# Layer 0 with y kept by channels, and an order drawn up in finer steps

## The chip, the core and the metric

The kernel runs on one core of a Trainium2 chip. A core has five engines with instruction queues of their own: TensorE (PE; its weight loads are shown apart as PEld), VectorE (DVE), ScalarE (ACT), GpSimd (POOL) and SyncE (SP), which issues the DMA transfers. Each engine works through its queue in the order of the program and waits on semaphores. The metric is the device time of one execution in microseconds (us).

## The reference

The input x has 8 images of 64 x 64 positions and 192 channels. Two layers follow one another, each of the form x + layer(groupnorm(x)). Layer 0, the only one that the change touches, is a state-space block. Cut to what matters:

```python
xs = x + dwconv2d(x)                        # 3x3, by channel
h  = layernorm(xs)
z, xBC, dt = split(h @ in_proj_w.T)         # 384, 384+64+64, 6
xBC = silu(causal_conv1d(xBC))              # 4 taps
y  = ssd(xm, softplus(dt), A, Bm, Cm)       # 6 heads of 64, state 64
y  = (y + xm * D_skip) * silu(z)
y  = y * rsqrt(mean(y * y) + 1e-5) * rms_w  # mean over the 384 channels
x2 = xs + y @ out_proj_w.T
x2 = x2 + dwconv2d(x2)
out = x2 + gelu(layernorm(x2) @ fc1_w.T + fc1_b) @ fc2_w.T + fc2_b
```

`ssd` is a recurrence along the 4096 tokens of an image, worked out by chunks. Inside a chunk, y is a masked matrix of Cm and Bm products, weighted with exp of differences of a running sum `cs`, times x*dt. From the chunks before comes Cm times the carried state times exp(cs). Layer 1 is a scan over four directions; its code is the same in both kernels.

## The kernel before

All numbers are float32. `layer0` (from line 249) works in 64 tiles of 512 tokens, 8 for each image, and a tile has 4 chunks of 128 tokens. Data lie mostly with channels on the partitions: 128 channels as one 128 x 512 block, and the other 64 channels as two strips of 64 partitions, one for each half of the tokens, in a 128 x 256 block.

**Order.** Layer 0 is written as generators (`conv1`, `norm1`, `mix`, `convolve`, `gate`, `steps_in_time`, `decays`, `powers`, `scores`, `turn`, `states`, `mixer`, `output`, `conv2`, `norm2`, `mlp` and others), each of which walks over the tiles. A generator yields steps: an engine, a planned duration (the "weight", in us), a function that issues the instructions, and a time when the input is ready. The class `Flow` (line 150) is a list scheduler that runs while the program is built. It keeps one clock for each engine and always takes the step that can start earliest, plus 0.01 us times the rank of its generator (`RANKS0`). `f.keep` then fixes that order for each engine. Buffers are slots that a generator takes and gives back: five PSUM banks "mm", three "sm", five buffers "e", one each of "xdt", "xw" and "yc". `LAG` is added to each step's end. A step on ACT that needs another table of functions costs `TABLE` = 1.3 us more in the plan, and `STAY` shifts its place in the choice. So the planned weights decide what the engines' queues look like, and the chip then runs that order with its own durations.

**The part around the change**, for a tile:

- `gate` (L672, L683): z and dt by tokens. The normalised h is the stationary operand (128 tokens), the weights move (390 columns: 384 of z, 6 of dt). `keep_gate` adds the bias to dt on DVE (L700) and applies SiLU on ACT (L703) for each chunk.
- `steps_in_time` and `rows_of`: the running sums `cs` by tokens, and, turned, as rows `csr`, which go to DRAM (`csd`, L777). `decays` (L792) loads them back spread over 128 partitions into `e` (128 x 768 a chunk). `powers` turns `e` into exp(-relu(cs_i - cs_j)) with six activations and one (L805, L810), and `scores` multiplies it with the masked products of Bm and Cm (L834).
- `turn`: x by tokens through three transposes (L852), times dt (`xdt`, L858) and times the weight for the state (`xw`, L862).
- `states`: the part of y from the carried state. Two matmuls with Cm stationary (L911) give it by tokens, and DVE scales it by exp(cs) into `t1` (L920, twice a chunk). Then the new state: two matmuls (L938) and two DVE operations (L951, L954).
- `mixer`: y by tokens in one PSUM bank. Three matmuls with x stationary add x*D_skip (L977), six with `e` stationary (128 x 128) and `xdt` moving (64 columns) add the heads (L980). DVE adds `t1` (L993) and multiplies with silu(z) (L996), and ACT squares with a row sum (L1004).
- `output`: the root of the mean square by tokens (L1023, L1024), scaling (L1033), three transposes a chunk back to channels (L1040), a copy into `yc` (L1049), the output projection (L1064, and L287 for the last 64 channels), and on DVE the sum with xs (L1073).
- `mix` (`halves_of_pair`, L277 and L281), `output`, and `mlp` (`rows_of_pair`, L267 and L268; fc2 in L1180 and L287) hand PE one step each for a pair of banks or a whole projection, of 1.4 to 5.33 us by the plan.

## Time and profile before

| what | us |
|---|---|
| three runs of the kernel | 22291.52, 22295.5, 22308.64 (median 22295.5) |
| the profiled execution, its own time | 22303.65 |
| its span, from the first to the last instruction | 22301.9 |
| layer 0, about 75 to 4310 us of the span | 4235 |
| busy in that stretch: PE, DVE, ACT, POOL | 3892.10, 3459.95, 3076.69, 622.15 |

The page gives shares of the whole span, and four fifths of the span are layer 1. So for this change the stretch of layer 0 is read by itself, and its sums are divided by 64 to get times for a tile. Busy time on PE contains stretches in which its clock was granted at half, and there the same matmul shows twice its duration. A "row" of the groups shows the busy time of all instructions of one line and shape and the mean duration of one. Since matmuls overlap, busy time divided by the count is less than the mean duration. A float32 matmul shows as two records.

### The profile page before, as it was taken

To read this page: it belongs to the slowest core of one execution; us is meant where nothing else is said; L and a number is where in the kernel's file an instruction comes from. 1 tells how busy PE (TensorE), PEld (TensorE's weight loads), DVE (VectorE), ACT (ScalarE), POOL (GpSimd) and SP (SyncE) were. 2 spreads that over 40 slices of the span, in tenths; PEclk is the share of its full clock that TensorE was granted. 3 is DMA by queue.
4 is the path that set the end of the run, shared out by engine and by line. 5 is a ranking of instruction groups with operands and counts; after the bars stand their busy time and mean duration, and the time that the engine had idled before them with its cause. 6 is when DMAs were issued, how large, how long until landed. Compare 5 with 4: busy or idle time off the path is not lost. (4 is left out here: it accounts for less than half of the span.)

```text
span 22301.9 us, 358177 instructions
## 1 busy us (share of the span) xinstructions
PE 20993.5 (94%) x122600; PEld 11023.1 (49%) x122600; DVE 20777.7 (93%) x23205; ACT 19864.1 (89%) x35400; POOL 16103.8 (72%) x13412
## 2 busy tenths in 40 slices
PE   8999999799999999999999999999999999999999
PEld 5555555445544554455445544554455445544554
DVE  7888888799999999999999999999999999999998
ACT  6777777599989998999899989998899889988998
POOL 1111111189968996899689968997899789977997
PEclk8999999899999999999999999999999999999999
DMA  2111111233333333333333333333333333333332
GB/s 57 53 53 48 53 49 50 66 99 95 92 100 102 92 93 103 100 93 94 100 101 95 95 97 103 95 94 94 106 94 93 93 109 93 95 91 109 95 95 75
DMA packets 1732538, 1957.50 MB, mean 88 GB/s; under 512 B 551472, under 2 KB 1077712, under 8 KB 1721488
## 3 DMA queue, kind: packets, MB, share of 16 engines
q1 hardware_dynamic: 1730704, 1934.58, 31.5%
q8 instruction: 963, 15.78, 0.3%
q14 instruction: 871, 7.14, 0.1%
HBM read 1318.69 MB, written 212.60 MB: 69 GB/s over the span
## 5 line engine op out<-in xcount | busy, mean ns | idle before, releaser
L1959 POOL TENSOR_TENSOR hs<-hs,cb 128x1024 f32<-128x1024 f32 x6144 | 14589.7, 2375 | 497.7 <-POOL cy L1957 5.4
L1945 DVE TENSOR_TENSOR_SCAN hs<-ea,cy,g 128x512 f32<-128x512 f32 x10752 | 12915.9, 1267 | 188.2 <-PE g L1929 164.8
L1903 ACT ACTIVATE ea<-dr,an 128x512 f32<-128x512 f32 x12288 | 8158.2, 712 | 455.5 <-DVE hs L1945 406.0
L1894 ACT ACTIVATE pw<-duT,bt 128x384 f32<-128x384 f32 x14304 | 7840.5, 604 | 12.1 <-DMA xo<-xt 6.1
L1974 PE MATMUL y<-hs,sel 128*64 128x512 f32 x24576 | 6635.5, 618 | 353.9 <-POOL hs L1959 335.0
L1929 PE MATMUL g<-ident,pw 128*128 128x128 f32 x43008 | 6099.6, 281 | 70.0 <-DVE hs L1945 26.6
L1929 PEld LDWEIGHTS g<-ident,pw 128*128 128x128 f32 x43008 | 4614.9, 141 | 2558.0 <-issue 1254.1
L1917 PEld LDWEIGHTS g<-dg,duT 128*64 128x64 f32 x24576 | 1556.8, 136 | 2062.7 <-issue 1503.1
L1957 POOL COPY cy<-hs 128x2 f32<-128x2 f32 x6144 | 1160.9, 189 | 1901.7 <-DVE hs L1945 1863.2
L1917 PE MATMUL g<-dg,duT 128*64 128x128 f32 x24576 | 2256.5, 282 | 178.7 <-DVE hs L1945 106.1
L1974 PEld LDWEIGHTS y<-hs,sel 128*64 128x64 f32 x24576 | 1234.2, 135 | 1564.6 <-issue 865.1
L1945 DVE TENSOR_TENSOR_SCAN hs<-ea,g 128x512 f32<-128x512 f32 x1536 | 1754.4, 1203 | 161.3 <-PE g L1929 114.6
L500 POOL TENSOR_TENSOR s<-s,sq 64x256 f32<-64x256 f32 x256 | 221.7, 866 | 1878.3 <-ACT sq L494 1839.1
L1413 DVE SCALAR_TENSOR_TENSOR xs<-pad,p,xs 128x2048 f32<-128x2048 f32 x384 | 899.8, 2350 | 130.7 <-ACT xs L1397 120.8
L1808 PE MATMUL p_dt<-xdbl,wd 13*128 13x512 f32 x1536 | 868.9, 646 | 94.8 <-DVE duT L1837 71.4
L1773 PE MATMUL p_d<-xc,wx 128*44 128x512 f32 x1536 | 797.5, 603 | 28.5 <-DMA xc<-xo 28.5
L1830 PEld LDWEIGHTS p_du<-ident,de 128*128 128x128 f32 x3072 | 324.6, 141 | 618.0 <-DVE de L1821 407.3
L1808 PEld LDWEIGHTS p_dt<-xdbl,wd 13*128 13x128 f32 x1536 | 226.7, 184 | 732.6 <-DVE duT L1837 292.7
L1837 DVE TENSOR_TENSOR duT<-p_du,ut 128x512 f32<-128x512 f32 x768 | 514.0, 670 | 2.0 <-PE p_du L1830 2.0
L1821 DVE SCALAR_TENSOR_TENSOR de<-spa,p_dt 128x512 f32<-128x512 f32 x768 | 509.4, 664 | 3.9 <-ACT spa L1816 3.9
L1816 ACT ACTIVATE spa<-spa 128x512 f32<-128x512 f32 x768 | 485.8, 632 | 24.4
L1830 PE MATMUL p_du<-ident,de 128*128 128x128 f32 x3072 | 502.6, 287 | 3.5 <-DVE de L1821 3.5
(305 smaller groups left out, 19724.3 us busy)
## 6 DMA issues: line engine op xcount, KB each, us to landing
cb<-cd SPq DMA_DIRECT2D x4096, 128.0 KB
dr<-de SPq DMA_DIRECT2D x3072, 128.0 KB
xc<-xo SPq DMA_DIRECT2D x256, 768.0 KB
dg<-dz SPq DMA_DIRECT2D x256, 512.0 KB
e<-csd SPq DMA_DIRECT2D x256, 384.0 KB
ut<-xo SPq DMA_DIRECT2D x128, 768.0 KB
ut<-xo SPq DMA_DIRECT2D x256, 384.0 KB
xo<-xs SPq DMA_DIRECT2D x48, 1024.0 KB
```

The source lines that it names most:

```text
L1413: nc.vector.scalar_tensor_tensor(xs, tap(d, h, j), kw[:, d, j : j + 1], xs, ALU.mult, ALU.add)
L1773: nc.tensor.matmul(st["p_d"][:44], wx[:, d, k], st["xc"][:, d], start=d == 0, stop=d == DT - 1)
L1808: nc.tensor.matmul(ps, st["wd"][32:45, d * 128 : d * 128 + 128], xds[s % 2][32:45], start=True, stop=True)
L1830: nc.tensor.transpose(pt[:, j * 128 : j * 128 + 128], st["de", d][:, j * 128 : j * 128 + 128], ident)
L1894: o(nc.scalar.activation(to, what, AF.Copy, scale=by))
L1903: nc.scalar.activation(ea[:, f], state[s]["dr", d][:, f], AF.Exp, scale=an[:, k, p, at : at + 1])
L1917: nc.tensor.matmul(gs[f][i * 64 : i * 64 + 64, j * 128 : j * 128 + 128], state[s]["duT"][:, j, (2 * d + f) * 64 : (2 * d + f) * 64 + 64], ...
L1929: nc.tensor.transpose(gs[f][:, j * 128 : j * 128 + 128], state[s]["pw", p, j][:, 2 * d + f].rearrange("p a b -> p (a b)"), ident,)
L1945: nc.vector.tensor_tensor_scan(rev(h[:, f]), rev(ea[:, f]), rev(g[f]), 0.0 if first(s) else state[s - 1]["cy"][:, p, d, f : f + 1], ALU.mu ...
L1957: o(nc.gpsimd.tensor_copy(st["cy"][:, p, d], h[:, :, last]))
L1959: o(nc.gpsimd.tensor_mul(h, h, bc(st["cb", p], 1, [128, 2, TT])))
L1974: o(nc.tensor.matmul(y[half[f]], sel, hc[:, f], start=p == ORDER[0] and k > 0, stop=p == ORDER[-1]))
```

## The change

Layer 0 now keeps y by channels from the start, and the planner is given finer steps and other numbers. For a tile:

- z is computed by channels like the other rows (`halves_of_pair` for the first 256 rows, `single` for the last 128 and, with h stationary, for the six columns of dt).
- y comes out by channels: for each head `xdt` is stationary (64 columns) and `e` moves (128 columns), two heads side by side on the two halves of the PSUM partitions. The part of the carried state is added in the same bank: the state is stationary (64 x 64), and `ec` moves, which is Cm times exp(cs). `ec` is loaded like `e` (two more DMAs a chunk, from exp(cs) that ACT adds to `csr`) and multiplied with Cm on DVE.
- x*D_skip is made on ACT (`cvd`, three operations a tile), and DVE adds it and multiplies with silu(z) straight into `yc`. The transposes, the scaling by tokens and the copies into `yc` go.
- The mean square is now over partitions: ACT squares half a tile, a matmul with ones sums, and Ln and Exp run on 128 x 512 (`ry`). Since it comes after the projection, DVE multiplies p_o with `ry` and then adds xs.
- PE steps of `mix`, `gate`, `output` and `mlp` are split (`in_parts`), and the six activations of `powers` are six steps.
- Planned weights, `LAG` (0.3 to 0.35), `STAY` (-0.7 to -0.98) and all ranks but four are other numbers, so the whole order of layer 0 is drawn up anew.

```diff
-    mlp=8, norm2=-26, conv2=18, output=-48, mixer=5, states=-10, turn=-21, scores=7, powers=41, decays=-99,
-    steps_in_time=-25, convolve=-14, mix=-3, gate=3, norm1=-15, conv1=16, inputs=3, statistics=46, stay=-0.7,
+    mlp=8, norm2=-13, conv2=15, output=22, mixer=-1, states=7, turn=-21, scores=7, powers=24, decays=274,
+    steps_in_time=-7, convolve=12, mix=37, gate=0, norm1=-15, conv1=-10, inputs=41, statistics=-112,
+    stay=-0.98,
...
+    def in_parts(parts, ready):
+
+        for weight, part in parts:
+            r = yield step("PE", weight, part, ready)
+            ready = 0.0
+        return r
...
+        of, weight, size = (rest_of, 0.46, 3) if few else (main_of, 0.89, 1)
+        return [(weight * size, lambda k=k: of(range(k, k + size))) for k in range(0, n, size)]
...
-                1.3,
+                1.75,
                 lambda: [
                     nc.gpsimd.tensor_add(s2[two[g], half[g]], s2[two[g], half[g]], sq[two[g]]) for g in range(2)
...
+                yield "take", "cvd"
+                cvd = got["cvd", T] = tp.tile([128, 3, TT], F32, name="cvd")
+                for i in range(3):
...
+                        lambda: [nc.scalar.activation(cvd[:, i], cv[:, i], AF.Copy, scale=v128["dsk"][:, i : i + 1])],
...
+                            out.append(nc.tensor.matmul(at, wia[:, cols], main(h)[:, half[g]], start=True, stop=False))
+                        for c in range(NQ):
+                            at = ps[c // 2][:, TB + c % 2 * NH : TB + c % 2 * NH + NH]
...
+                            out.append(nc.tensor.matmul(at, h[:, tk], wia[:, DIN : DIN + NH], start=False, stop=False))
...
+                    parts = ((2.6, single),) if last else halves_of_pair(ps, wia, wib, h, cols)
...
+            r = yield step("ACT", 0.24, lambda: [nc.scalar.activation(csr[:, 1], ps[: NQ * NH, :Q], AF.Exp)], None, "explog")
...
+                        out = [nc.sync.dma_start(out=e, in_=src)]
+                        for i in range(2):
+                            by = csd[c * NH + i : c * NH + NH : 2, 1].partition_broadcast(NS)
+                            out.append(nc.sync.dma_start(out=ec[two[i]], in_=by))
...
+                            "DVE", 0.49, lambda: [nc.vector.tensor_mul(ec, ec, bc(cm[:, tk], 1, [128, NH // 2, Q]))]
...
-                                nc.tensor.matmul(pi[i][:, :HC], queries[i][:, tk], st[two[i]], start=True, stop=True)
...
-                        for hd in range(NH):
-                            cs = slice(hd * HD, hd * HD + HD)
-                            f.keep(nc.tensor.matmul(py[:, cs], e[:, hd], xdt[:, cs], start=False, stop=hd == NH - 1))
...
+                        for j in range(3):
+                            for i in range(2):
+                                hd = 2 * j + i
...
+                                        py[two[i], j * 128 : j * 128 + 128],
+                                        xdt[:, hd * HD : hd * HD + HD],
+                                        e[:, hd],
...
+                                        py[two[i], j * 128 : j * 128 + 128],
+                                        st[two[i], j * HD : j * HD + HD],
+                                        ec[two[i], j],
...
-                    q = yield step("PE", 2.35, out)
+                    q = yield step("PE", 1.7, out)
...
+                    q = yield step("DVE", 0.5, lambda: [nc.vector.tensor_add(yc[:, :, tk], v(py), cvd[:, :, tk])], q)
+                    f.give("sm", q)
+                    q = yield step("DVE", 0.53, lambda: [nc.vector.tensor_mul(yc[:, :, tk], yc[:, :, tk], zs[:, :, tk])])
...
+            r = yield step("ACT", 0.83, lambda: [nc.scalar.activation(ysq, yc[:, :, half[g]], AF.Square)], r)
...
+                    nc.tensor.matmul(ps[:, half[g]], ones1, ysq[:, j], start=j == 0, stop=j == 2) for j in range(3)
...
+                            lambda: [nc.vector.tensor_mul(inner[at], im(ps[at, : n * WI]), im(ry[at, tk]))],
...
+                        "DVE", (0.64, 0.38)[i], lambda: [nc.vector.tensor_add(inner, inner, im((main, rest)[i](xs)))]
```

## The prediction

> **What bounds the kernel now.** I read the sums of busy time by stretches first, because the page mixes two layers. Columns: stretch, length, then busy us (and instructions) of PE, PEld, DVE, ACT, POOL, then the granted PE clock, DMA share, GB/s.

> ```profile
> 75.00:4310.00 4235.00, 3892.10 (x18524) 2272.61 (x18523) 3459.95 (x7131) 3076.69 (x6233) 622.15 (x1049) 0.92 0.17 49
> 500.00:4200.00 3700.00, 3416.43 (x16395) 1990.03 (x16396) 3071.76 (x6325) 2723.93 (x5520) 553.89 (x928) 0.93 0.17 50
> 4300.00:4400.00 100.00, 61.61 (x209) 29.86 (x208) 64.95 (x47) 47.13 (x51) 3.33 (x8) 0.77 0.38 119
> ```

> Layer 0 takes 4235 us, 66.2 for each of 64 tiles. In a tile PE is busy 60.8, DVE 54.1, ACT 48.1, POOL 9.7. PE bounds, but loosely: it idles 5.4 us a tile, and its clock averages 0.92. The timeline of PE shows what the clock does (start, duration, line, records; in brackets the idle time before):

> ```profile
> 2024.92 2.82 PE L980 MATMUL p_y<-xdt,e 128*128 128x64 f32 x12 [0.76 <-DVE e L834]
> ...
> 2048.07 0.83 PE L977 MATMUL p_y<-dsk,cv 128*128 128x128 f32 x6
> 2048.74 1.45 PE L980 MATMUL p_y<-xdt,e 128*128 128x64 f32 x12
> 2050.12 0.28 PE L867 MATMUL p_b<-ident,bm 64*128 64x64 f32 x1
> ...
> 2051.11 2.81 PE L287 MATMUL p_f<-m,wf 128*64 128x256 f32 x24
> ...
> 2065.26 1.99 PE L277 MATMUL p_x<-h,wia 128*128 128x256 f32 x8
> 2067.18 1.13 PE L281 MATMUL p_x<-h,wib 64*128 64x256 f32 x8
> 2068.24 1.12 PE L474 MATMUL ln_m<-x,ones 128*128 128x512 f32 x2
> ```

> The six heads take 1.45 us at one time and 2.82 at another, shortly after an idle time of 3.23 us (before L741 at 2021.41): PE works at half rate now and then. At 0.92 of the clock, 60.8 busy us hold about 56 of full-rate work. So three terms make the period: 56 us of work, 5 lost to half rate, 5 idle. Idle time comes from the others, and DVE in turn waits for PE (who waits for whom, DVE, 500 to 4200 us: total us, times, longest):

> ```profile
> DVE xdt L858 <- PE p_y L980: 162.1, 84, 5.5
> DVE st L954 <- PE p_n L938: 53.1, 44, 4.3
> DVE h L482 <- PE ln_m L476: 51.6, 45, 5.9
> DVE t L920 <- PE p_i L911: 40.0, 37, 4.7
> DVE cv L636 <- ACT cv L621: 39.2, 20, 11.0
> ```

> All lines of that view with a PE step on the right add to 507 us, 9.1 a tile, three quarters of DVE's idle 12.1. The two engines hold each other up in a fixed order, with PE the longer.

> **PE, part by part** (full-rate durations, as distances between starts in the timeline).

> y and the carried state go first. Now a chunk costs 2.05 (2048.07 to 2050.12) and 0.48 for the two L911 products (four records, 0.16 apart by pairs); the other PSUM step of `states` stays. After: three pairs with 64 stationary columns and 128 moving. The nearest row is L287, pairs of the same shape with 256 moving columns: 24 records, six pairs, 2.74 us to the next start, so 0.457 a pair and 0.23 for 128 columns. Three pairs of heads are 0.69. Pairs for the state (64 rows to 64 columns) have no row: between 0.23, both at once, and 0.43, one after the other (a 128-column matmul is half of L476's 0.43 for 256). I take 0.23, as in L281 and L287 where halves of the array run together. The sum is 1.38, and 1.5 with a tail: 1.0 saved a chunk, 4.1 a tile. The other end is 2.1 to 2.3, which saves 1 to 1.8.

> The transposes L1040 go: 142.2 us of busy time for 256 chunks, 0.56, at full rate 0.5; 2.0 a tile.

> z: now two pairs of 2.45, 4.9. After, one pair as in `mix`, 2.98 (2065.26 to 2068.24), and `single`: half of that for its four 256-column matmuls, 1.49, and eight tiny ones. Four have 128 stationary columns, as L741, whose starts lie 0.22 apart: 0.88. The four strips I put at 0.15 (0.05 to 0.22): 0.6. Sum 5.95, so 1.05 more (0 to 1.3).

> The sums of squares are new: six 256-column matmuls of 0.43 as L476, 2.6 more.

> Sum: -4.1 - 2.0 + 1.05 + 2.6 = **-2.45 us of PE work a tile**, bounds -3.9 and +0.2. Splitting steps issues no instruction more.

> **DVE.** These rows carry it:

> ```profile
> L920 DVE TENSOR_TENSOR t<-p_i,dec 128x192 f32<-128x192 f32 x496 | 172.0, 351 | 45.2 <-PE p_i L911 43.9
> L996 DVE TENSOR_TENSOR yt<-yt,zs 128x384 f32<-128x384 f32 x248 | 152.5, 615 | 0.8
> L1073 DVE TENSOR_TENSOR xx0a<-p_o,xs 128x512 f32<-128x512 f32 x22 | 15.2, 692 | 41.3 <-PE p_o L1064 41.2
> L1073 DVE TENSOR_TENSOR xx0b<-p_o,xs 128x256 f32<-128x256 f32 x22 | 9.3, 424 | 8.4 <-PE p_o L287 8.3
> ```

> L920 goes, 172.0/64 = 2.7. `ec` times Cm has the shape of L996: 0.49 (half of L834, 980 ns) to 0.615, four times, 2.1. Behind the projection there was one sum, 0.69 + 0.42; after, a product in three pieces, 0.69 + 2 x 0.42, and then the sum: 1.5 more. dt: two additions for four, 0.15 less. The others keep their shapes. Net **+0.8: DVE 54.9**.

> **ACT.** Away: scaling 158.2, copies 121.8, squares with their sums 182.3, roots 32.2, in all 494.5/64 = 7.7. New: three `cvd` of about 0.7 (0.618 for 384 elements in L1033), two squares of 0.84 (as L810), Ln and Exp 1.3 (L512, L513), a second Cm 0.63, exp 0.25, z 0.2: 6.2. Net -1.5, ACT 46.6. A fall in `STAY` lets the planner change tables sooner; one load more a tile (1.28 us, 5.5 now) stays under ACT's 18 us of slack.

> **The rest at nothing, and its cover.** SP issues eight DMAs more a tile, 0.37 each as in L792, and two more chunk loads bring half as many bytes again; ACT waits 28.1 us for `e` in 56 tiles now, and if every wait doubled that is 0.5 a tile on ACT's slack, or 32 us in all without it. POOL's copies of the `cin` head wait for the banks of the tile before; POOL is busy 15%, and `mix` alone is queued behind. "mm" gives one bank to the squares for about two chunks; "sm" is taken five times a chunk instead of eight. `yc` has one buffer and is now taken at the start of `mixer`: the next tile's DVE sums queue behind this tile's last projection matmul, about 4 us of PE once in 66, against three more tiles' work in other generators. Who would be late if that shows is DVE, which is the rival below.

> Finer steps and new ranks have no row: they can save part of the 5.4 idle and the 5 at half rate, or add to them. The planned weights move towards the rows (POOL's sums 1.3 to 1.75, shown 2 x 0.866; its copies 0.8 to 1.05, shown 2 x 0.517), which speaks for a small gain. I take none.

> **Forecast**: 2.45 x 64 = 157 off the profiled execution's 22303.65, 22147; the median lies 8 lower, so **22140**. It holds if idle time and half rate stay as they are. Own range 22060 to 22230. Chance 0.43.

> **Rivals.**

> - *More.* With PE less loaded and in pieces, a quarter to a third of DVE's 9.1 goes too, 2.5 more a tile: 4.9 x 64 = 314 off, 21980. For it: four of the five longest waits end in a PE step. Against: xdt has one buffer still. 0.13.
> - *Half the gain goes to the clock.* From 0.923 busy to 0.616 the mean clock goes from 0.93 to 0.77, 0.5 of clock for each 1.0 of busy share. If PE's freed time turns to idle, 58.4 of 65 us busy instead of 60.8 of 66.2, the clock falls by 0.01, which is 0.7 us, and with some idle left 1.2 of 2.45 remain: 77 off, 22220. 0.12.

> [...]

> - *Nothing is left.* If the state pairs run one after the other (0.43 each) and the tiny matmuls cost 0.22, y is 2.2 and z 6.2: PE keeps 56 us, and the time is 22280. 0.12.

> [...]

> - *Slower: DVE takes over.* Place: its queue around xdt, y and the projection. If its waits are not shortened by PE's relief, because xdt and yc have one buffer each and their chain is the same length, the period is DVE's 54.9 + 12.1 = 67.0, 0.8 more: 51, or 22350 beside the median. It decides once PE's period, 66.2 less its saving, falls under that sum, which it does with any saving at all; so it hangs on the waits alone. For it: DVE at 83% of the period is close behind. Against: most of its waits name PE steps that get shorter. A badly drawn order would show here too. 0.20.

> **Range and chances.** 0.2% is about what a measurement can tell from no change, 45 us. More, forecast and the half gain are faster: 0.68, less 0.02 for the edges; nothing left is 0.13, slower 0.21. The range must take in the first rival and most of the last: 21960 to 22370.

> **What would show it.** Layer 0's end near 4155 in place of 4310. Right: y's busy time a chunk (2.58 now with both rows) falls to about 1.7; the state pairs start together; DVE's sum is 3510 in layer 0; PE's clock stays 0.92. Wrong if the state pairs start 0.1 us apart or more, if DVE idles 12 us a tile with PE's share under 0.88, or if ACT's waits for `e` exceed 2 us a tile. Layer 1, about 17990 us, must not move.

## The result and the profile after

The changed kernel takes 21974.96 us (median, 21962.79 to 21974.97), the kernel before 22298.75 in the same comparison: a ratio of 0.9853, interval 0.9836 to 0.987. That is 324 us less, where 155 were forecast. The profiled execution has a span of 21972.1 us.

Busy time of the changed kernel in layer 0, which now ends at 3982 us (columns as in the prediction):

```profile
75.00:3982.00 3907.00, 3614.18 (x20489) 2095.71 (x20487) 3527.94 (x6944) 3024.08 (x5667) 617.53 (x1049) 0.97 0.25 66
```

A tile takes 61.0 us instead of 66.2. PE's clock averages 0.97 where it was 0.92, and DVE is busy 90% of the time (it was 82%). The rest of the span is 17990 us, before 17993: all of the difference is in layer 0. The waits of DVE in the changed kernel, 500 to 3900 us:

```profile
DVE xdt L917 <- PE p_y L1013: 97.1, 97, 5.0
DVE h L503 <- PE ln_m L497: 49.1, 44, 4.4
DVE st L980 <- PE p_n L963: 12.3, 17, 4.3
DVE gm L885 <- PE p_g L881: 11.2, 17, 4.4
DVE yc L1042 <- PE p_y L1024: 10.7, 7, 5.1
```

All lines of that view with PE on the right add to 217 us in 55.7 tiles, 3.9 a tile instead of 9.1. Now the new y on PE, in the timeline of the changed kernel:

```profile
2033.80 0.88 PE L1013 MATMUL p_y<-e,xdt 128*64 128x128 f32 x12
2034.60 0.87 PE L1024 MATMUL p_y<-ec,st 64*64 64x128 f32 x12
2035.40 1.98 PE L304 MATMUL p_f<-m,wf 128*128 128x512 f32 x4
```

Heads and state take 0.80 each from start to start, 1.6 a chunk.

To compare versions I split a tile of layer 0 into three terms of PE, from all its records and the granted clock at each moment: **work** (busy time times clock), **half-rate loss** (busy time times one minus the clock) and **idle** time. The three add up to the period. Some matmul records are missing, so differences of 0.3 us in work mean little. The terms are rounded one by one.

| kernel | median us | period | work | half-rate loss | idle | DVE busy |
|---|---|---|---|---|---|---|
| before | 22298.75 | 66.2 | 56.4 | 4.5 | 5.4 | 54.1 |
| changed | 21974.96 | 61.0 | 54.8 | 1.7 | 4.6 | 55.1 |

Of the 5.1 us less, only 1.6 are work. 2.8 are half-rate loss and 0.8 idle time.

### The profile page after: what moved, and what is told of

It reads as the page before. It is cut to its first block, busy times and chain, and to the rows that moved or that the text cites. A ratio compares the mean times of both kernels' runs of the same rounds, so it can differ in the third digit from the quotient of the medians.

```text
span 21972.1 us, 362013 instructions
## 1 busy us (share of the span) xinstructions
PE 20709.3 (94%) x124584; PEld 10850.2 (49%) x124584; DVE 20850.1 (95%) x23026; ACT 19801.9 (90%) x34834; POOL 16081.9 (73%) x13412
## 5 line engine op out<-in xcount | busy, mean ns | idle before, releaser
L862 ACT ACTIVATE e<-e,cst 128x128 f32<-128x128 f32 x1536 | 567.2, 393 | 36.2 <-DMA e<-csd 34.4
```

The costliest lines, as they stand in the source:

```text
L862: nc.scalar.activation(e[:, h], e[:, h], AF.Relu, bias=cs[:, c, h : h + 1], scale=-1.0)
```

## The experiments

Three theories were tested. WORK: the time follows PE's work. ORDER: it follows the order that the planner draws (finer steps, ranks, weights). And, formed from the first eight runs, STREAM: PE's clock follows how long columns stream, and y by channels streams better. By streaming I mean the time that a matmul's moving columns take, without waits for weights. Ratios are to the kernel before, timed on the same chip as each group of versions (medians 22300.28, 22304.9, 22302.51 and 22301.08).

**Less work in the same order**

```diff
-                        for i in range(3):
-                            cs = slice(i * 128, i * 128 + 128)
-                            f.keep(nc.tensor.matmul(py[:, cs], cv[:, i, tk], dsk[:, i], start=i == 0, stop=False))
```

> The kernel before, same order on every engine, without the three matmuls a chunk that add x*D_skip (the output lacks that term). PE has 4 x 0.67 = 2.7 us of full-rate work less a tile, more than the change takes away (1.6 by the two traces). Theory WORK (one for one, as the prediction's sum): 64 x 2.7 = 171 less, about 22130. Theory DOUBLE (less work also wins back half-rate time): 300 or more less, under 22000. Theory ORDER (the waits are fixed by the order and the freed time turns into idle time): less than 80 off, 22220 to 22300, with PE's idle time a tile up from 5.3 towards 8 us.

Measured: 22237.95 us, ratio 0.997 (0.996 to 0.9981). Its busy times in layer 0:

```profile
75.00:4240.00 4165.00, 3759.57 (x16985) 2114.19 (x16982) 3455.50 (x7128) 3071.55 (x6233) 622.33 (x1049) 0.91 0.17 50
```

Work falls by 2.7 to 53.6 us a tile, and the period by 1.1: idle time rises to 6.3 and half-rate loss to 5.1. WORK and DOUBLE fall. The time is within what ORDER named, though idle time rose to 6.3 and not towards 8. In this order, 62 of the 171 us of work taken away reach the time; the rest went to idle time (1.0 a tile) and to half rate (0.6).

**Parts of the change, with the ranks that are at hand.** Finer steps alone, in the kernel before:

```diff
-                    p = yield step("PE", (5.33, 2.7)[i], project, r)
+                    p = yield from in_parts(sums_of(ps, wf2, m, 6, i), r)
```

> The kernel before with y by tokens, its own ranks and planned weights, but the PE steps of mix, the output projection, fc1 and fc2 and the six ReLUs of powers as separate steps. No instruction is added or removed. Theory ORDER by finer steps: 150 to 250 off, 22050 to 22150, and the half-rate time of a tile falls from 10 to 7 us or less. Theory WORK: no change but for the chance of another order, 22240 to 22360.

Measured: 22522.3, ratio 1.0099 (1.0084 to 1.0114). Both theories missed: the kernel got slower by 222 us. Half-rate loss is 5.3, idle time 7.3.

Coarse steps again, in the changed kernel:

```diff
-        for weight, part in parts:
-            r = yield step("PE", weight, part, ready)
-            ready = 0.0
+        r = yield step("PE", sum(w for w, _ in parts), lambda: [i for _, part in parts for i in part()], ready)
```

> The changed kernel with its ranks and weights, but each pair or projection on PE and the six ReLUs again as one step. Same instructions as the changed kernel. Theory ORDER by finer steps: 150 to 250 of the 324 are lost, 22120 to 22230. Theory WORK: it stays near 21975, within 60.

Measured: 22434.9, ratio 1.0061 (1.0044 to 1.0077), 460 us above the changed kernel and far outside both expectations. Its busy times in layer 0 hold the instructions of the changed kernel in 4360 us instead of 3907, with 9.8 us of idle time and 4.0 of half-rate loss a tile:

```profile
75.00:4435.00 4360.00, 3732.19 (x20488) 2188.89 (x20486) 3551.19 (x6943) 3097.39 (x5726) 612.12 (x1049) 0.92 0.22 59
```

The old ranks in the changed kernel:

```diff
-    mlp=8, norm2=-13, conv2=15, output=22, mixer=-1, states=7, turn=-21, scores=7, powers=24, decays=274,
+    mlp=8, norm2=-26, conv2=18, output=-48, mixer=5, states=-10, turn=-21, scores=7, powers=41, decays=-99,
...
```

> The changed kernel with finer steps and its weights, but the ranks and STAY of the kernel before. Same instructions but for the number of table loads. If the new ranks carry the gain, 100 or more are lost: 22080 and up. If finer steps or less work carry it, within 60 of 21975.

Measured: 22277.77, ratio 0.9991 (0.9981 to 1.0). 303 of 324 us are lost with the same work, as expected if the ranks carry the gain. So no part with borrowed ranks gives a clear gain: two of the three versions are slower than the kernel before, by 222 and 135 us. This does not yet say that finer steps are worth anything: the ranks of one plan were used in another.

**The same parts, each with ranks of its own.** I searched ranks for each set of steps until the planner's own plan was shortest, and ran the result, one search for each version. The edit is the dictionary of ranks alone, besides what is named.

> The changed kernel with coarse steps again, and with ranks of its own, found by a search for the shortest plan of these steps. Same instructions as the changed kernel. If finer steps are needed for the gain: 22060 to 22160. If any steps do once the ranks are drawn for them: within 50 of 21975, and the coarse run with borrowed ranks (22435) was slow for its ranks alone.

Measured: 22000.19, ratio 0.9864 (0.9847 to 0.988). Coarse steps with ranks of their own are 25 us behind the changed kernel; the rest of the coarse run's 22435 came from its ranks.

> The kernel before (y by tokens, coarse steps) with the planned weights and LAG of the changed kernel for the steps that both have, and ranks found by the same search. If better weights and a new search carry the gain: 22150 or less. If y by channels is needed: 22230 to 22330.

Measured: 22221.77, ratio 0.9961 (0.9947 to 0.9976), between the two expectations and 8 us from the second: new weights and a search give 83 us, not the whole gain.

> The kernel before (y by tokens) with finer steps, the new planned weights and ranks found by the search for these steps. If finer steps carry the gain once they have ranks of their own: 22100 or less. If y by channels is needed too: 22250 to 22400, still under the 22522 of finer steps with borrowed ranks.

Measured: 22273.06, ratio 0.9987 (0.9978 to 0.9996). With y by tokens, finer steps bring nothing; this order is 51 us slower than the coarse one at 22222.

To tell the search from the weights in the run at 22222:

> The kernel before with its own planned weights and LAG, and ranks found by the search from its own as a start. It separates the search from the weights in the run with both (22222). If the search carries those 80: 22210 to 22240. If the weights nearer to the trace do: 22270 to 22310.

Measured: 22203.51, ratio 0.9955 (0.994 to 0.997), a little under what the search was expected to carry.

> The kernel before with the new planned weights and LAG, but its old ranks. If weights nearer to the trace help by themselves: 22220 to 22270. If ranks fit only the weights that they were drawn for: 22350 to 22550, as in the runs with borrowed ranks (22278, 22435, 22522).

Measured: 22358.39, ratio 1.0026 (1.0016 to 1.0036). So the search alone gives 98 us, with the old weights. Weights nearer to the rows gave nothing here: with old ranks they cost 57 us, and with searched ranks the run that has them is 18 us slower (22222 against 22204).

> The changed kernel with seven ranks a little different (decays 154 for 274, mix 36 for 37, inputs 43 for 41, statistics -111 for -112), whose plan is as long as its own within 0.03%. It shows how far orders with the same work and the same length on paper lie apart on the chip. If the plan's length carries the time: within 15 of 21975. If orders scatter: 30 or more off, and then 25 us for finer steps (22000 against 21975) says nothing.

Measured: 21970.31, ratio 0.9852 (0.9837 to 0.9866). The edit changes the four ranks that are named, not seven. This neighbour lies within 5 us. But it is a near copy of one order, and two searches can end further apart: with y by tokens, searched orders lie at 22204, 22222 and 22273, and there the finer steps are the slowest. So it is not shown that the 25 us come from finer steps.

**What y by channels adds.** With searched ranks on both sides and coarse steps, y by tokens takes 22203.51 and y by channels 22000.19: 203 us, 3.1 a tile. The version by channels also has the new planned weights and LAG, which gave nothing above; with them on both sides the difference is 222 us. Work differs by 1.5 of the 3.1, half-rate loss by 1.6 (3.6 against 2.0), idle time by nothing (4.9 and 4.8). Layer 0 by tokens, then by channels:

```profile
75.00:4209.00 4134.00, 3821.36 (x18522) 2249.71 (x18521) 3438.71 (x7128) 3091.18 (x6250) 607.61 (x1049) 0.94 0.18 50
75.00:4008.00 3933.00, 3623.96 (x20534) 2135.67 (x20532) 3578.11 (x6946) 3024.91 (x5682) 629.56 (x1051) 0.96 0.25 66
```

Why does the clock differ at equal idle time? In layer 0 of both kernels' traces the granted clock is recorded as 1.00 or 0.50, and every stretch at one value is a multiple of 3.41 us long (174 records before, 106 in the changed kernel). Four stretches of 3.41 us of the kernel before, and PE's timeline in them:

```profile
1480.38:1483.79 3.41, 2.74 (x16) 1.61 (x14) 3.38 (x7) 3.38 (x8) 0.33 (x2) 1.00 0.00 0
1483.79:1487.20 3.41, 2.14 (x15) 1.84 (x15) 2.16 (x5) 2.29 (x8) 0.00 (x0) 1.00 0.00 0
1487.20:1490.62 3.42, 1.32 (x5) 0.85 (x5) 3.39 (x9) 0.88 (x3) 0.00 (x0) 0.50 0.00 0
1490.62:1494.03 3.41, 3.41 (x5) 1.34 (x5) 1.83 (x4) 3.39 (x6) 0.00 (x0) 0.50 0.00 0
```

```profile
1484.15 1.55 PE L980 MATMUL p_y<-xdt,e 128*128 128x64 f32 x12 [0.67 <-DVE e L834]
1485.63 0.27 PE L867 MATMUL p_b<-ident,bm 64*128 64x64 f32 x1
1486.81 0.49 PE L825 MATMUL p_g<-cm,bm 64*128 64x128 f32 x2 [0.91 <-DVE xw L862]
1488.83 0.88 PE L1040 MATMUL p_u<-ident,yt 128*128 128x128 f32 x3 [1.53 <-DVE yt L993]
```

PE is busy for 2.14 of 3.41 us in the second stretch, and the clock is halved behind it (0.50 after 1.00). Most of that busy time is L980, which moves 64 columns behind 128 weight columns: 12 records of 64 columns stream for 0.65 us (an estimate, 0.84 ns a column and record, from the 12 records of 512 columns of L1180 in the 5.15 us between 2042.06 and 2047.21), out of 1.48. I counted such streaming time for all stretches of 3.41 us between 500 and 4200 us (3880 in the changed kernel) that had the full clock:

| | before: stretches, then halved | changed |
|---|---|---|
| columns stream under half of the stretch | 84, 63 | 39, 35 |
| more | 852, 8 | 899, 6 |
| PE busy for 0.5 to 0.75 of it | 91, 42 | 53, 5 |

At the same busy share the kernel before loses its clock in 42 of 91 cases and the changed one in 5 of 53. Streaming separates the cases in both; busy time does so less well.

These counts add up the columns of matmuls that run side by side, such as L287's, whose pairs start 7 ns apart. Counted once, as the time in which any column streams, the separation is sharper. Under 0.4 of the stretch, 65 of 72 are followed by half rate in the kernel before and 39 of 44 in the changed one; above it 6 of 865 and 2 of 895. Over the traces of all seventeen versions, under 0.4 it is 970 of 1036, and from half of the stretch on 1 of 14340. The 0.4 was chosen after the counts, to divide these stretches; so divided, 156 of all 15993 lie on the wrong side, and 414 if they are divided by busy time, at the share (0.56) that suits the two kernels best.

To try streaming by itself, y by tokens was made to stream more and save nothing:

```diff
-                            cs = slice(hd * HD, hd * HD + HD)
+                            cs = slice(hd // 2 * 128, hd // 2 * 128 + 128)
```

> The kernel before, same order and number of instructions, but each head's matmul in y moves 128 columns instead of 64 behind the same 128 weight columns: the columns of both heads of a pair, so that y also gets products of one head with the other's x (that is what the output has wrong). Nothing is saved; PE streams 6 x 64 columns more a chunk, under its weight loads. Theory STREAM (the clock is halved after windows in which columns stream for less than about half of the time, and weight-bound matmuls count as little): half-rate loss falls from 4.5 us a tile to 3 or less, and the time by 60 to 200, to 22100 to 22240. Theory IDLE (the clock goes by the idle time between matmuls): no gain, 22290 to 22400.

Measured: 22236.2, ratio 0.997 (0.9959 to 0.9982). In its timeline and its sums:

```profile
2022.36 0.83 PE L977 MATMUL p_y<-dsk,cv 128*128 128x128 f32 x6
2023.03 1.50 PE L980 MATMUL p_y<-xdt,e 128*128 128x128 f32 x12
2024.46 0.28 PE L867 MATMUL p_b<-ident,bm 64*128 64x64 f32 x1
```

```profile
75.00:4240.00 4165.00, 3819.17 (x18515) 2230.84 (x18515) 3452.34 (x7126) 3072.60 (x6233) 618.18 (x1048) 0.95 0.17 50
```

The step is no shorter (1.43 us to the next start, before 1.38), the columns are twice as many, idle time stays (5.4 both times), and half-rate loss falls from 4.5 to 3.0. The kernel gets faster by 66 us while PE does more arithmetic. STREAM holds in this run, at the small end of what it named, and IDLE falls. Stretches at half rate go down from 146 of 1083 to 102 of 1054.

> The same edit in y by tokens with the new weights and its own searched ranks (22222). Theory STREAM: 22020 to 22160, most of the way to y by channels with coarse steps and its own ranks (22000). Theory IDLE: 22210 to 22320.

Measured: 22170.32, ratio 0.994 (0.9927 to 0.9954), against 22221.77: 51 us. Half-rate loss 2.8 (4.2). The direction holds, the size was guessed too large: set against the 222 us between 22222 and 22000, streaming more columns in the heads' step gives about a quarter. The rest is 1.6 us of work a tile and another 0.8 of half-rate loss, for which I have no run. The transposes and the state products, which the change also takes away, were not tried one by one.

**Who sets the period now**

```diff
-                    q = yield step("DVE", 0.23, lambda: [nc.vector.tensor_mul(gm, pg[:, :Q], up)], q)
+                    q = yield step("DVE", 0.23, lambda: [nc.vector.tensor_mul(gm, pg[:, :Q], up) for _ in range(2)], q)
```

> The changed kernel, same order, with the product of scores and mask done twice on DVE: 4 x 0.284 = 1.14 us of DVE work a tile more, 73 in all. If DVE sets the period of the changed kernel: 60 to 110 later, 22035 to 22085. If PE or the fixed order does: 30 or less.

Measured: 22004.73, ratio 0.9865 (0.985 to 0.988): 30 of 73 us.

```diff
+                    nc.tensor.matmul(ps[:, half[g]], ones1, ysq[:, 0], start=True, stop=True)
+                ]
+                + [
                     nc.tensor.matmul(ps[:, half[g]], ones1, ysq[:, j], start=j == 0, stop=j == 2) for j in range(3)
```

> The changed kernel, same order, with the first of the three matmuls of each half's sum of squares done twice: 2 x 0.43 = 0.86 us of PE work a tile more, 55 in all. If PE still sets the period one for one: 22020 to 22040. If DVE and PE share it, as 1.14 us more on DVE (30 of 73) suggests: 15 to 35 later, 21990 to 22010.

Measured: 22006.95, ratio 0.9866 (0.9851 to 0.9881): 32 of 55 us. DVE passes on 0.4 of what it is given and PE 0.6. Neither sets the period alone.

```diff
-("xdt", 1), ("xw", 1)
+("xdt", 2), ("xw", 2)
```

> The changed kernel with two buffers each for xdt and xw instead of one, and ranks found by the same search for these slots. The longest wait of DVE (xdt for p_y) goes. If the plan's gain of about 1% of layer 0 reaches the chip: 21920 to 21950. If the clock or DVE eats it: 21960 to 22000.

Measured: 21967.57, ratio 0.9849 (0.9835 to 0.9862), 7 us under the changed kernel, no more than `after_near` without second buffers. DVE's longest wait did not go:

```profile
DVE xdt L917 <- PE p_y L1013: 110.1, 77, 4.9
DVE h L503 <- PE ln_m L497: 26.8, 31, 4.3
```

Why it stayed with a second buffer was not followed up. No version here beats the changed kernel clearly.

The terms of all versions, in us a tile, sorted by time:

| version | median us | period | work | half-rate loss | idle | DVE busy |
|---|---|---|---|---|---|---|
| changed, two buffers, own ranks | 21967.57 | 61.0 | 54.9 | 1.7 | 4.3 | 55.5 |
| changed, near ranks | 21970.31 | 61.0 | 54.8 | 1.7 | 4.5 | 55.1 |
| changed, coarse, own ranks | 22000.19 | 61.4 | 54.6 | 2.0 | 4.8 | 55.9 |
| changed, more DVE | 22004.73 | 61.4 | 54.9 | 1.7 | 4.8 | 56.2 |
| changed, more PE | 22006.95 | 61.6 | 55.6 | 1.7 | 4.3 | 55.2 |
| tokens, own ranks and new weights, wide | 22170.32 | 64.0 | 56.2 | 2.8 | 5.0 | 54.0 |
| tokens, own ranks, old weights | 22203.51 | 64.6 | 56.1 | 3.6 | 4.9 | 53.7 |
| tokens, own ranks, new weights | 22221.77 | 64.9 | 55.9 | 4.2 | 4.8 | 54.0 |
| before, wide | 22236.2 | 65.1 | 56.7 | 3.0 | 5.4 | 53.9 |
| before, no skip term | 22237.95 | 65.1 | 53.6 | 5.1 | 6.3 | 54.0 |
| tokens, finer, own ranks, new weights | 22273.06 | 65.9 | 56.7 | 3.5 | 5.7 | 53.5 |
| changed, old ranks | 22277.77 | 65.8 | 54.7 | 3.7 | 7.4 | 55.5 |
| before, new weights | 22358.39 | 67.0 | 56.3 | 4.6 | 6.1 | 53.9 |
| changed, coarse | 22434.9 | 68.1 | 54.3 | 4.0 | 9.8 | 55.5 |
| before, finer | 22522.3 | 69.6 | 57.0 | 5.3 | 7.3 | 53.9 |

## Why the prediction was right in sign and wrong in size

The failed step is the one that carried the forecast: "It holds if idle time and half rate stay as they are", with "Finer steps and new ranks have no row [...] I take none". What was set at zero there measured 3.6 us a tile (2.8 of half rate, 0.8 of idle time), 230 us. It is not all the order's doing. Along the path of runs at the end of this section, half rate goes from 4.5 to 3.6 with a new search, to 2.0 with y by channels and to 1.7 in the changed kernel. The prediction had no clock term for y itself. The term that I did size, PE's work, was too large: 1.6 and not 2.45. The two errors have opposite signs, so that the forecast still named about half of the gain is partly luck; had the work alone counted, the gain would have been about 100 us at best, and the run without the skip term shows that even this is not passed on in a given order.

By the steps:

- *PE's terms.* y costs 1.6 a chunk (1.5 taken). The squares and z cost more. By busy time a tile, the little half-rate time included, the squares take 196.7 us in 64 tiles, 3.1 (2.6 taken), and z 6.4 (5.95 taken): its rows sum to 125.7 + 72.7 + 70.3 + 45.0 + 61.0 + 32.6 = 407.3 us. Two of these rows of the changed kernel:

```profile
L1069 PE MATMUL p_q<-ysq,ones 128*128 128x256 f32 x768 | 196.7, 393 | 9.2 <-ACT ysq L1057 9.0
L706 PE MATMUL p_z<-h,wia 128*128 128x256 f32 x256 | 70.3, 394 | 2.3 <-ACT m L1173 1.9
```

- *Bounds.* The sum's upper bound of +0.2 does not follow from the ends that it names: -1 for y, -2.0 for the transposes, +1.3 for z and +2.6 for the squares make +0.9.
- *Signs.* y's busy time fell to 1.74 us a chunk, the state pairs start together and DVE's sum is 3528, as named. The clock did not stay at 0.92: it rose to 0.97, and that is the step above.
- *DVE*: 54.9 forecast, 55.1 measured; the product of `ec` takes 601 ns, as L996 did (615). *ACT*: 46.6 forecast, 47.3 measured. *The cover*: ACT waits 33.9 us for `e` in 55.7 tiles (28.1 in 55.9 before). These held.
- *Rival "more"* gave the right time, 21980, by luck, and half of its mechanism: DVE's waits for PE fall by 5.2 us a tile, twice what was priced, while the work that it adds them to was too large. Pieces are not the reason: with coarse steps and ranks of their own the waits are 3.0 us a tile. Nor are searched ranks alone: with y by tokens they leave 8.5 of 9.1. Nor is y by channels alone: with old ranks 5.8 remain. The waits fall where y by channels and ranks of its own come together.
- *Rival "half the gain goes to the clock"* had the sign wrong for this change. PE's busy share stayed (0.92 and 0.93) and the clock rose. The slope that I took from 0.77 at 0.616 mixed the end of layer 0 with its middle. The run without the skip term does go that way: less work, more half-rate loss.
- *Rival "nothing is left"*: the state pairs take 0.80 us for three, as the heads' pairs do, and the two of a pair start 7 ns apart, so they run together: 0.27 us a pair, while they write two halves of the partitions of one bank; one after the other would be 0.43, by an estimate from the 256 columns of L476. The rival's time was wrong by its own figures too: y at 2.2 a chunk and z at 6.2 make 0.6 us more a tile, about 22335 and not 22280.
- *Rival "slower"*: DVE did come up to 90% of the period, but its waits were shortened. Such a price comes back in the versions with borrowed ranks, where DVE has the same work and idles up to 12.6 us a tile.

How the 324 us divide, along one path of runs: 98 for a new search of ranks with the old steps (22301 to 22204), 203 for y by channels with ranks of its own and the new weights (to 22000), and 25 from there to the changed kernel, which may be finer steps or the luck of a search (to 21975). That makes 326; the kernel before differed by 2 us between the groups of versions. More columns in the heads' step gained 51 to 66 us in two orders of y by tokens. That is what the runs show of the clock's part in the 203; the rest of it is argued from the terms. Another path would divide differently.

## What to carry to other kernels

Where a planner fixes the order of the engines, take its steps, weights and ranks as one thing: compare parts of a change only after ranks were drawn anew for each, or the order's part hides the rest (460 us here against 25). Price the clock as a term of its own: here idle time stayed at 5.4 us a tile and work within 0.3 (56.4 and 56.7), while the half-rate loss moved by 1.5 (4.5 to 3.0). Where a matmul's moving side is shorter than its weights, try the longer operand on the moving side: here 128 moving columns for 64 went with a mean clock of 0.95 for 0.92 in layer 0, at nearly the same duration of the step (1.43 us for 1.38).
